# Moving the inner sums of the keys' seventh product to the end of the opening's queue

## Chip, cores and metric

The kernel runs on one core of one Trainium2 chip. The metric is the device time of one execution in microseconds (us); the times given are the median of the runs of one kernel, and one further execution is taken apart by the profiler.

## What is computed

`x` holds 8 images of 512 channels by 1024 positions (fp32). Two attention layers follow each other, each with a residual sum:

```python
# layer 0: LayerNorm over channels, 8 heads of 64
q, k, v = (xn @ W.T + b for each of Wq, Wk, Wv)
x = (softmax(q k^T / 8) v) @ Wo.T + bo + x
# layer 1: GroupNorm of 32 groups, one head of 512
q, k, v = (W h + b for each of wq, wk, wv)
x = x + wp (softmax(q^T k / sqrt(512)) v) + bp
```

The 512x512 weights are the same for all images.

## The kernel before

**Products.** The 512-wide matrix products are done as 2x2 blocks in Winograd's form of Strassen's scheme, with seven block products in place of eight. `STEPS` lists the seven; each needs a block of the weights or a sum of blocks (S1 to S4). Some products are done so twice: the block itself is cut into 2x2 again ("deep"), and then its own inner sums are needed. For the weights these inner sums are made once, in the opening (the work before the first attention), by `save_deep_later`. It queues five pieces for each group of slots: four VectorE additions and one transfer, on the queue of GpSimd (POOL), of the result to DRAM (`saved_deep`). Groups 0, 1 and 2 hold two slots each, and group 3 only one, slot "22", which is the operand of the seventh product. From the second image on `load_deep` reads these sums back; for the keys (`"k"`) that is all four groups.

**The queue of small work.** Instructions are laid down in the order in which the Python code runs; within one engine they run in that order. Small work is put into a queue, `side`, with `later`. A `Product` step lays down its matmuls (`multiply`), then takes `pieces` pieces off the front of `side` (`tick`), then lays down its evictions (`leave`). `Pair.values` takes one piece for each of its eight key blocks. `until` takes pieces until a condition holds. So the place of a piece in `side` decides where its instructions stand among those of the main work.

**The next image's layer norm.** `LayerNorm(1)` is cut into pieces by a generator, `steps`: two sums over channels on VectorE (`lns`), a matmul with ones for the mean (L1045, into a PSUM bank), four ScalarE copies to `mu` (L1063), four subtractions (L1107), four squares on ScalarE (L1111), sums of the squares (`lnq`), a matmul for the variance (L1045, into a PSUM bank named `var`), a VectorE transpose that reads this bank out (`vart`, L990), the inverse root, its spread (`rstd`, L995) and four multiplications (L1135). `queue` puts the first piece at the end of `side`; each piece then puts its successor at place 1, that is, behind one other piece:

```python
side.insert(len(side) if self.waiting == "now" else 1, piece)
```

**The opening around the change.** The keys of image 0 (`project("k0")`) are followed by its queries (`project("q0")`, two units of seven steps), its values (`project_v("v0")`, two units of seven steps), and then the first two score stages. With the queries, the keys' inner sums are queued (20 pieces), three steps are done, and `ln.queue()` is called; the inner sums of the queries' (`q`), and of two combined weights (`a`, `m`), are queued ahead of the values.

**Scores and values of layer 0.** For a pair of heads, `Pair.scores` lays down, for each of eight key blocks, two matmuls (L1294) that fill 128x1024 of PSUM, an exponential on ScalarE (`p`, L1297), and a running sum on VectorE (`sum`, L1301 and L1303). `Pair.values` multiplies with the values (L1312, into `acc`), and the result is copied out on ScalarE (L1316). Two pairs' scores are followed by two pairs' values. `PairSums.take` folds the sums with transfers on POOL (L1005, L1001).

**Buffers.** PSUM is split into three wide tiles of two banks (`wide_psum`) and two single ones (`bank`). Three of a double pair's sixteen score blocks use the two single banks, one for each half, in place of a wide tile:

```python
if m + self.c % 2 * NM in (7, 11, 15):
    s = None
    parts = [bank(f"s{i}_{self.tag}_{m}") for i in range(2)]
```

The single banks also hold the `y` of each product unit, the mean and the variance. Tiles of 128x1024 in SBUF come from a pool of 46 (`big_tile`), tiles of 128x512 from a pool of 9 (`half_tile`). A tile comes free when the last instruction laid down that uses it is done.

Of the kernel before, what the change touches and what calls it, by code (L numbers as in the profile page):

```python
# [71 lines left out]
def fast_path(ctx: ExitStack, tc: tile.TileContext, x: bass.AP, vecs: dict, weights: dict, out: bass.AP,  # L72
# [32 lines left out]
    def big_tile(name):  # L105
        return big.tile([P, S], F32, tag="b", name=name)

    def half_tile(name):
        return half.tile([P, HB], F32, tag="h", name=name)
# [40 lines left out]
    def load_x(b):  # L150
        t = {}
        for k in range(NH):
            for j in range(2):
                t[j, k] = block(f"x_{b}_{j}{k}")
                nc.sync.dma_start(out=t[j, k], in_=x[b, ts(j, CB), ts(k, HB)].rearrange("(a p) t -> p a t", p=P))
        return t
# [57 lines left out]
    def deep_tile(n, b, g):  # L214
        return big_tile(f"w_{n}_{b}_{g}_deep").rearrange("p (s i o) -> p s i o", s=2, i=4)
# [10 lines left out]
    def save_deep_later(n, w, groups=range(3)):  # L226

        def sums(g):
            s = len(SLOTS[2 * g : 2 * g + 2])
            left, right = w[g][:, :s, :, :P], w[g][:, :s, :, P:]  # L230
            made = []

            def one(i, l, r, op):
                if not made:
                    made.append(deep_tile(n, "first", g))
                d = made[0][:, :s]
                l, r = (d[:, :, x] if isinstance(x, int) else x for x in (l, r))
                nc.vector.tensor_tensor(d[:, :, i], l, r, op)

            later(lambda: one(0, right[:, :, 0], right[:, :, 1], ALU.add),  # L240
                  lambda: one(2, left[:, :, 0], right[:, :, 0], ALU.subtract),
                  lambda: one(1, 0, left[:, :, 0], ALU.subtract),
                  lambda: one(3, left[:, :, 1], 1, ALU.subtract),
                  lambda: nc.gpsimd.dma_start(out=saved_deep[n][:, g, :s], in_=made[0][:, :s]))

        for g in groups:
            sums(g)
# [35 lines left out]
    def first_w(n):  # L283
        w = weight_tiles(f"{n}_first")
        load_blocks(n + "0", w)
        return w
# [7 lines left out]
    wk_now, wq_now = first_w("k"), first_w("q")  # L294
# [57 lines left out]
    def later(*work):  # L352
        side.extend(work)
# [116 lines left out]
    def banks_of(tag, r, shared, own="x"):  # L470

        def banks(to):
            if to == "y":
                return bank(f"y_{tag}_{r}")
            if shared is None or to in own:
                return wide_psum(f"{to}_{tag}_{r}")[:, :HB]
            if to not in shared:
                shared[to] = wide_psum(f"{to}_{tag}")
            return shared[to][:, ts(r, HB)]
        return banks  # L480
# [9 lines left out]
    def token_part(r):  # L490

        def part(dst, a, b, opens):
            for m in range(2):
                for k in range(2):
                    nc.tensor.matmul(dst[:, ts(m, CB)], b[:, k, ts(2 * r + m, P)], a[:, k, :],  # L495
                                     start=(opens and m == 0 and k == 0), stop=(k == 1), skip_group_check=True)
        return part
# [458 lines left out]
    def project_v(tag, w, h, apart=False):  # L956


        res, shared = {}, None if apart else {}

        def unit(r):
            def dest(i, k):
                if (i, k) not in res:
                    res[i, k] = big_tile(f"{tag}_{i}{k}")
                return res[i, k][:, ts(r, HB)]

            return Product(f"{tag}_{r}", w, h, token_part(r), plain_shift, dest, banks_of(tag, r, shared))
        return [unit(r) for r in range(2)], res
# [728 lines left out]
    with tc.manual_schedule(engines=ORDERED):  # L1697
# [56 lines left out]

        units, qt = project("q0", wq_now, bias_of("bq0"), hb)
        ln.xt = load_x(1)
        save_deep_later("k", wk_now, range(4))
        units[0].step(3)
        ln.queue()
        for u in units:  # L1760
# [2 lines left out]
        save_deep_later("q", wq_now)  # L1763
        save_deep_later("a", wa, (1, 2))
        save_deep_later("m", wm, (1, 2))
        units, vts = project_v("v0", wv_now, hb)
        units[0].pieces = 0
        units[0].step(1)
# [3 lines left out]
        for b in range(B):  # L1772
# [13 lines left out]
            for i in range(HEADS):  # L1786
# [3 lines left out]
                p = pairs[i]  # L1790
# [524 lines left out]
@with_exitstack  # L2315
def attn_block_x2(ctx: ExitStack, tc: tile.TileContext, x: bass.AP, vecs: dict, weights: dict, out: bass.AP):
    nc = tc.nc
    keep = ctx.enter_context(tc.tile_pool(name="keep", bufs=1))
    flag = keep.tile([1, 1], I32, tag="flag", name="flag")
    fast_path(tc, x, vecs, weights, out, flag)  # L2320
    left = nc.values_load(flag[0:1, 0:1])
    with tc.If(left > 0):
        general_path(tc, x, vecs, weights, out)
# [39 lines left out]
```

## Time and profile before

| | |
|---|---|
| median of 3 runs | 2793.82 us (2792.96 to 2796.17) |
| profiled execution, its own time | 2795.6 us |
| its span in the trace | 2793.9 us, so 1.7 us lie around the span |
| TensorE busy | 2777.7 us (99% of the span) |
| VectorE, ScalarE, GpSimd busy | 2177.2, 1274.0, 523.1 us |
| mean granted TensorE clock | 0.998 |

The trace gives each instruction's start, its duration and what released it. PE is TensorE's matmuls, PEld its weight loads, DVE is VectorE, ACT ScalarE, POOL GpSimd, SP the engine that issues most loads. Ends of matmuls are modelled, so intervals are best taken from start to start. Every fp32 matmul is shown as two rows. Engines that are not the bottleneck may be idle at no cost.

### The profile page before, as it was taken

The page shows a single profiled execution, that of the slowest core. Times are in us where ns is not written, and L with a number is a line of the kernel's source. Part 1 is how long each engine was busy: PE and PEld are TensorE (multiplying, and loading weights), DVE is VectorE, ACT ScalarE, POOL GpSimd, SP SyncE. Part 2 cuts the span into 40 slices and gives each one's busy share as a digit, 9 for nine tenths or more (in the row PEclk, how much of TensorE's full clock was granted, in tenths as well). Part 3 has the DMA queues.
Part 4 walks back from the last instruction along what each step waited for, and adds up shares of the span by engine and source line. Part 5 has one row for each costly group of instructions (what it writes and reads, how often), then busy time and mean ns, then how long its engine had stood idle before and what let it go on. Part 6 is the DMA issues. An engine that isn't in the chain of part 4 may idle for free.

```text
span 2793.9 us, 32794 instructions
## 1 busy us (share of the span) xinstructions
PE 2777.7 (99%) x11385; PEld 1637.5 (59%) x11385; DVE 2177.2 (78%) x3128; ACT 1274.0 (46%) x2152; POOL 523.1 (19%) x719
## 2 busy tenths in 40 slices
PE   9999999999999999999999999999999999999999
PEld 4534766357663585536855468644676447763375
DVE  6687798678877788777887778777887778757776
ACT  4463435634357243562436534365344743336342
POOL 2022012210222102221022210222012210122001
PEclk9999999999999999999999999999999999999999
DMA  8235458344673537636475364744548434282223
GB/s 310 100 101 132 133 128 215 76 125 125 162 189 67 156 109 189 150 74 176 111 194 117 83 192 118 197 88 105 165 121 208 97 103 132 61 215 63 66 91 96
DMA packets 143550, 372.96 MB, mean 133 GB/s; under 512 B 20064, under 2 KB 24464, under 8 KB 143376
## 3 DMA queue, kind: packets, MB, share of 16 engines
q0 software_dynamic: 58208, 141.34, 26.9%
q1 hardware_dynamic: 81040, 216.56, 22.3%
q10 hardware_dynamic: 4128, 12.87, 1.5%
q8 instruction: 92, 1.51, 0.2%
q14 instruction: 82, 0.67, 0.1%
HBM read 208.43 MB, written 64.75 MB: 98 GB/s over the span
## 4 chain that ended last, share of the span: by engine, by line
PE 99%; ACT 0%; DMA 0%; DVE 0%; issue 0%; SPq 0%; DVEq 0%
PE acc L1312 16%; PE s L1294 16%; PE x_o L511 8%; PE s L1460 7%; PE x_v L495 4%; PE y_o L511 4%; PE x_out L486 4%; PE y_s L1460 3%; PE y_v L495 2%; PE c_vm L858 2%; PE s L1495 2%; PE y_out L486 2%; PE z_o L511 2%; PE x_k L609 2%; PE x_q L609 2%; PE c_qa L732 2%
## 5 line engine op out<-in xcount | busy, mean ns | idle before, releaser
L1303 DVE TENSOR_TENSOR sum<-sum,p 128x1024 f32<-128x1024 f32 x384 | 470.4, 1225 | 40.4 <-ACT p L1297 2.2
L1297 ACT ACTIVATE p<-s 128x1024 f32<-128x1024 f32 (+1 forms) x608 | 479.3, 980 | 20.2 <-PE s L1294 20.2
L1312 PE MATMUL acc<-p,v_again 128*64 128x512 f32 x1792 | 390.9, 594 | 0.0
L1312 PEld LDWEIGHTS acc<-p,v_again 128*64 128x64 f32 x1792 | 126.1, 137 | 261.3 <-issue 236.7
L1001 POOL DMA_DIRECT2D fold<-sum x312 | 207.4, 752 | 338.1 <-DMA sum<-sum 212.1
L1294 PE MATMUL s<-q,k 64*128 64x512 f32 x1152 | 253.7, 593 | 4.5 <-ACT p L1297 4.5
L1301 DVE TENSOR_TENSOR sum<-p,p 128x1024 f32<-128x1024 f32 x64 | 78.1, 1221 | 156.0 <-ACT p L1297 156.0
L1294 PE MATMUL s<-q_lower,k_lower 64*128 64x512 f32 x896 | 196.1, 592 | 0.0
L1294 PEld LDWEIGHTS s<-q,k 64*128 64x128 f32 x1152 | 109.8, 186 | 144.8 <-issue 86.0
L1294 PEld LDWEIGHTS s<-q_lower,k_lower 64*128 64x128 f32 x896 | 85.4, 186 | 110.4 <-issue 68.3
L1005 POOL DMA_DIRECT2D sum<-sum x78 | 63.5, 839 | 425.2 <-DVE sum L1303 199.3
L1316 ACT COPY o<-acc 128x512 f32<-128x512 f32 x63 | 36.9, 586 | 221.0 <-PE acc L1312 220.8
L1500 DVE TENSOR_TENSOR p<-p,p 128x1024 f32<-128x1024 f32 x96 | 112.9, 1216 | 6.3 <-ACT p L516 6.3
L511 PE MATMUL x_o<-T_p,S_vm 128*128 128x512 f32 x256 | 114.0, 592 | 0.0
L516 ACT COPY u(0, 0)_v<-x_v 128x512 f32<-128x512 f32 x16 | 9.4, 586 | 187.6 <-PE x_v L495 187.6
L486 PE MATMUL x_out<-T_o,w_o 128*128 128x512 f32 x192 | 89.2, 594 | 0.0
L511 PEld LDWEIGHTS x_o<-T_p,S_vm 128*128 128x128 f32 x256 | 48.6, 190 | 60.7 <-issue 60.7
L1358 ACT COPY rr<-r 32x16 f32<-32x16 f32 x256 | 53.2, 208 | 63.1 <-DVE r L1261 59.7
L495 PE MATMUL x_v<-w_v,T_h 128*128 128x256 f32 x336 | 80.0, 381 | 0.0
L995 DVE STREAM_TRANSPOSE rden<-rr 128x512 f32<-128x512 f32 (+1 forms) x72 | 53.4, 758 | 24.0 <-ACT rr L1603 15.2
L495 PEld LDWEIGHTS x_v<-w_v,T_h 128*128 128x128 f32 x336 | 63.3, 190 | 11.3 <-issue 3.3
L1448 ACT ACTIVATE p<-p 128x1024 f32<-128x1024 f32 x64 | 65.3, 1061 | 0.0
(680 smaller groups left out, 5609.5 us busy)
## 6 DMA issues: line engine op xcount, KB each, us to landing
sum<-sum POOLq DMA_DIRECT2D x78, 256.0 KB, 3.4
fold<-sum POOLq DMA_DIRECT2D x312, 64.0 KB, 2.3
x<-in_x_dram SPq DMA_DIRECT2D x32, 512.0 KB, 5.8
xr<-in_x_dram SPq DMA_DIRECT2D x64, 256.0 KB, 4.3
x_away<-x SPq DMA_DIRECT2D x32, 512.0 KB, 3.2
v_away<-v SPq DMA_DIRECT2D x28, 512.0 KB, 2.8
v_again<-v_away SPq DMA_DIRECT2D x28, 512.0 KB, 7.1
w_o<-saved_o SPq DMA_DIRECT2D x24, 512.0 KB, 5.1
```

The source lines that it names most:

```text
L486: nc.tensor.matmul(dst, a[:, k, ts(r, P)], b[:, k, :], start=(opens and k == 0), stop=(k == 1), skip_group_check=True)
L495: nc.tensor.matmul(dst[:, ts(m, CB)], b[:, k, ts(2 * r + m, P)], a[:, k, :], start=(opens and m == 0 and k == 0), stop=(k == 1), skip_grou ...
L511: nc.tensor.matmul(dst, a[:, r, ts(m, P)], b[m // 2][:, m % 2, :], start=(opens and m == 0), stop=(m == NM // 2 - 1), skip_group_check=True)
L609: nc.tensor.matmul(dst[:, ts(s, CB)], a[s], b[s], start=(opens and s == 0), stop=True, skip_group_check=True)
L1001: nc.gpsimd.dma_start(out=f[ts(q + i, BL), :], in_=t[ts(n, BL), ts(i, HB)], accum_op=ALU.add if n else ALU.bypass)
L1294: nc.tensor.matmul(parts[i], self.k[m // 4][r, ts(m % 4, P)], self.q[r, :], start=True, stop=True)
L1297: nc.scalar.activation(dst, src, AF.Exp, scale=1.0 / float(D) ** 0.5)
L1301: nc.vector.tensor_add(self.sum, self.p[0], p)
L1303: nc.vector.tensor_add(self.sum, self.sum, p)
L1312: nc.tensor.matmul(acc[i * D : (i + 1) * D, :], value_of(self.vt, m, self.c * P + i * D, D), self.p[m][:, ts(i, HB)], start=(m == 0), stop ...
L1460: nc.tensor.matmul(dst[:, ts(c, CB)], x[0][:, ts(c, P)], a[0], start=(opens and c == 0), stop=True, skip_group_check=True)
L1500: nc.vector.tensor_add(wide(t), wide(t), wide(x))
```

## The change

The keys' group 3 is taken out of the first call of `save_deep_later`, and a call of its own is put behind those of `q`, `a` and `m`. Its sums go into a half tile (128x512, from the pool of 9) where before they took half of a tile from the pool of 46. The same four additions and the same transfer are done.

```diff
@@ save_deep_later
                 if not made:
-                    made.append(deep_tile(n, "first", g))
+                    made.append(deep_tile(n, "first", g) if s == 2 else
+                                half_tile(f"w_{n}_first_{g}_deep").rearrange("p (s i o) -> p s i o", s=1, i=4))
                 d = made[0][:, :s]
@@ the opening
         ln.xt = load_x(1)
-        save_deep_later("k", wk_now, range(4))
+        save_deep_later("k", wk_now)
         units[0].step(3)
         ln.queue()
...
         save_deep_later("q", wq_now)
         save_deep_later("a", wa, (1, 2))
         save_deep_later("m", wm, (1, 2))
+        save_deep_later("k", wk_now, (3,))
         units, vts = project_v("v0", wv_now, hb)
```

## Prediction

> **What bounds the kernel now.** I read the page's busy times and chain first: TensorE is at work for 99% of the span, so an edit can gain only where TensorE waits or runs slowly.
>
> ```profile
> PE 2777.7 (99%) x11385; PEld 1637.5 (59%) x11385; DVE 2177.2 (78%) x3128; ACT 1274.0 (46%) x2152; POOL 523.1 (19%) x719
> PE 99%; ACT 0%; DMA 0%; DVE 0%; issue 0%; SPq 0%; DVEq 0%
> ```
>
> The waits of TensorE come next (total, times, longest). Nearly half of the 9.4 us that they hold in the whole span is one kind: scores that wait for an exponential.
>
> ```profile
> PE s L1294 <- ACT p L1297: 4.5, 3, 1.7
> PE pst_k L306 <- DMA w_k<-in_L_conv_wk_dram: 2.0, 1, 2.0
> ```
>
> TensorE's timeline puts all three into the first score stage, at 131, 136 and 141 us. The next score stages have none.
>
> ```profile
> 122.67 1.08 PE L1045 MATMUL var<-lnq,ones_c 128*64 128x512 f32 x4
> 123.68 7.13 PE L1294 MATMUL s<-q,k 64*128 64x512 f32 x30
> 131.92 3.70 PE L1294 MATMUL s<-q,k 64*128 64x512 f32 x16 [1.11 <-ACT p L1297]
> 137.33 3.70 PE L1294 MATMUL s<-q,k 64*128 64x512 f32 x16 [1.71 <-ACT p L1297]
> 142.75 1.12 PE L1294 MATMUL s<-q,k 64*128 64x512 f32 x2 [1.71 <-ACT p L1297]
> 143.80 15.65 PE L1312 MATMUL acc<-p,v 128*64 128x512 f32 x64
> 159.38 14.00 PE L1294 MATMUL s<-q,k 64*128 64x512 f32 x64
> ```
>
> A block is four rows, and the waits stand after rows 30, 46 and 62 of 64: in the middle of blocks 8, 12 and 16, the three that use the single banks, between their halves. VectorE's timeline says why only one bank is free. The variance is written at 122.67, but its reader comes only behind both pairs' running sums:
>
> ```profile
> 144.54 1.23 DVE L1303 TENSOR_TENSOR sum<-sum,p 128x1024 f32<-128x1024 f32 x1 [0.20 <-ACT p L1297]
> 145.68 0.71 DVE L990 STREAM_TRANSPOSE vart<-var 128x512 f32<-128x512 f32 x1
> ```
>
> So `var` holds one of two banks through the stage, and the second half of a block must wait for the exponential of its first half. The same work by stage (length; busy PE, PEld, DVE, ACT, POOL; granted clock; DMA):
>
> ```profile
> 123.68:143.80 20.12, 15.59 (x66) 6.20 (x65) 15.30 (x13) 14.90 (x18) 2.13 (x4) 1.00 0.32 99
> 143.80:159.38 15.58, 15.58 (x65) 4.89 (x65) 11.33 (x21) 1.72 (x4) 5.95 (x9) 0.89 0.53 127
> 159.38:173.31 13.93, 13.93 (x66) 6.10 (x64) 10.16 (x13) 13.34 (x17) 0.00 (x0) 1.00 0.00 1
> 173.31:187.20 13.89, 13.89 (x67) 4.51 (x65) 13.14 (x20) 4.30 (x13) 4.39 (x7) 1.00 0.45 78
> ...
> 144.00:146.00 2.00, 2.00 (x6) 0.48 (x4) 1.80 (x3) 0.50 (x1) 1.17 (x2) 0.53 0.49 53
> 146.00:148.00 2.00, 2.00 (x8) 0.62 (x6) 1.56 (x7) 0.54 (x2) 0.80 (x1) 0.62 0.41 49
> ```
>
> The first scores take 20.12 us against 13.93, and the values behind them 15.58 against 13.89: right after the waits the clock is granted at about half for some 4 us.
>
> [...]
>
> **The change part by part.**
>
> *Taken from the front of the queue.* Five pieces go: three additions of 0.283 us and one of 0.292 (128x128 rows of L238), 1.14 us of VectorE, and the POOL transfer issued at 90.80. None bounds TensorE. What counts is that the layer norm of image 1 stands behind twelve pieces where it stood behind seventeen, so all its pieces come five earlier. The instruction order of the changed program shows it: the mean's matmul moves ahead of four product steps (one y, x of the queries, x, z of the values), the variance's ahead of the last five steps of the values, and `vart` to before the scores. The number of matmuls is unchanged.
>
> *Are the moved pieces ready in time?* Worked from start times of before. VectorE begins `lns` at 89.49 instead of 90.42; four additions at paces of 1.15, 0.60, 1.15 and 0.68 end at 93.1. TensorE reaches the mean after the step at 92.05, plus 1.72: 93.8. Spare: 0.7. Image 1 was loaded from 32 us on, long landed. The `mu` copies start 1.15 after the mean (100.74 to 101.89 before), at 95.0, and the first subtraction 1.20 later at 96.2. ScalarE's squares now stand ahead of the copy `u(0, 0)_v`: squares at 97.4 and 99.2 (it waits for the second subtraction), the queries' copy, then `u(0, 0)_v`, done at 101.4. TensorE needs it at 93.8 + 1.1 (mean) + 4x1.72 = 101.8. Spare: 0.4, the tightest place. Further on, `v` block (1, 1) is added at 107.9 against 108.6, and `lnq` ends at 110.2 against 113.9. `var` ends at 115.0, `vart` at 115.8: eight us before the scores. I take 0 for new waits; the bounds are 0 and 1.5, as a late square holds back ScalarE's queue. Scores still start at 123.7, since the steps before them are the same ones.
>
> *The gain.* With both banks free the first stage is like the next: 20.12 - 13.93 = 6.19. Without the pauses I expect no half clock: 15.58 - 13.89 = 1.69. Sum 7.88. The next score stage then starts at 151.5 instead of 159.4.
>
> *What must keep up.* The sums are paced by VectorE (7.87 / 6 = 1.31 each): 14 of them from 126.8 to 145.2. Behind them stand three multiplications and one inner sum (4.0) and eight of `a` (3.4): 152.6. The next sums can start at 151.5 + 3.15 = 154.7. Spare 2. On POOL the first pair's folds stay; the second pair's end at 156.2 (issue of the last at 153.9, 2.3 to land). The changed program gives the buffer of that pair's sum to the exponential of pair 3's fifth block, due at 151.5 + 1.2 + 12x0.876 = 163.2 (ScalarE took 7.01 for eight). Spare 7.
>
> *Put at the end.* The four additions run at about 178. VectorE is busy 13.14 of 13.89 there, but three additions of `a` (1.25) leave that stage as these 1.14 come, and the stage behind has 3.8 to spare (10.16 of 13.93). The transfer (a POOL issue took 0.55) now stands behind those of `m` and ahead of pair 4's fold, where POOL sat idle 7.35. The half tile's next user is an eviction of the next image's values, past 230. No SP issue moves. I take 0 for it; bounds 0 and 0.5. If VectorE's slack were gone, 1.14 would fall on the sums. A later scaling (`rden`) stands behind two more pairs' sums; its reader is the projection after 242. Later images have the same order as before.
>
> **Rivals.**
>
> *Part of it.* The waits go, but the clock still dips, or the projections pay up to 1.5: gain 4.5 to 6.4, that is 2787.4 to 2789.3. For it: 0.4 us of spare is little. Against it: the other score stages all run at clock 1.00.
>
> *Slower.* The wait at 163.2: if the four folds of the second sum land late, ScalarE stops at pair 3's fifth exponential, and scores behind it. Each us past 163.2 costs one; it takes 171.1, fifteen us later than worked, to eat the gain. At 20 us late (176.2) it costs 13.0 - 7.9 = 5.1: 2798.9. For it: one fold waited 3.0 us for a transfer at 191. Against it: the longest chain seen, from the sum's issue at 183.05 to landing, is 12 us, and mine has 10.5 and 7 to spare.
>
> *Nothing happens.* ScalarE is the pace, not the bank: it was busy 14.90 of 20.12. Then 2793.8. Against it: 13.93 us are enough for the same exponentials one stage later.
>
> **How the numbers follow.** About 0.2% (5.6 us) is what a measurement of this kernel can tell from no change. Forecast as worked: 0.80; part of it: 0.12, of which 0.05 within 5.6 us; nothing: 0.04; slower: 0.04. So faster 0.87, same 0.09, slower 0.04. The profiled execution (2795.6, span 2793.9) would become 2787.7 and 2786.0. It is 1.8 above the median of 2793.82, which becomes 2785.9. The runs spread from 0.9 below to 2.4 above the median: 7.9 gained and 2 of spread give 2783.9; the worst of "part of it" gives 2789.3.
>
> **What would show it.** TensorE's waits without the line of scores on exponentials; the first score stage at 14 us; granted clock 1.00 in the values behind it; `vart` near 115. A wait of x of the values on ScalarE's copy near 102 would show the tight place failing; a wait on a fold near 163, the slower rival. I am wrong if the waits go and the stage stays at 18 us or more.

## The result, and the profile after

The changed kernel takes 2787.57 us (median of 12 runs, 2786.68 to 2789.31) against 2793.97 us for the kernel before (12 runs, 2792.96 to 2796.17): a ratio of 0.9976, 95% interval 0.9967 to 0.9985, or 6.4 us by the medians. Its profiled execution took 2787.6 us, with a span of 2785.9, against 2795.6 and 2793.9 before: 8.0 us. All lines of the new file stand one further down than before up to the place where the group was moved (scores L1295, values L1313, `vart` L991).

TensorE's busy time on the page, and then its waits in the whole span (total, times, longest):

```profile
PE 2774.7 (100%) x11385; PEld 1636.9 (59%) x11385; DVE 2177.2 (78%) x3128; ACT 1273.1 (46%) x2152; POOL 522.2 (19%) x719
```

```profile
PE pst_k L307 <- DMA w_k<-in_L_conv_wk_dram: 2.1, 1, 2.1
PE ps_first L1701 <- DVE checks L142: 1.3, 1, 1.3
PE pst_q L307 <- DMA w_q<-in_L_conv_wq_dram: 0.7, 1, 0.7
```

The line of scores that wait for an exponential, 4.5 us before, is gone; the longest that remain wait for the first weights and for the first tile of the program. TensorE did not compute less, its count of 11385 is the same. The timeline of TensorE, and below it VectorE's reader of the bank:

```profile
122.05 1.89 PE L496 MATMUL x_v<-w_v_first,T_h 128*128 128x256 f32 x8
123.87 14.00 PE L1295 MATMUL s<-q,k 64*128 64x512 f32 x64
137.81 13.95 PE L1313 MATMUL acc<-p,v 128*64 128x512 f32 x64
151.69 14.00 PE L1295 MATMUL s<-q,k 64*128 64x512 f32 x64
```

```profile
115.18 0.72 DVE L991 STREAM_TRANSPOSE vart<-var 128x512 f32<-128x512 f32 x1 [0.29 <-PE var L1046]
```

All 64 rows of the first score stage now run as one stretch, and the next score stage begins at 151.69 where it began at 159.38: 7.7 us earlier. `vart` is read eight us ahead of the scores and not in the stage behind them. The two stages by windows (length; busy PE, PEld, DVE, ACT, POOL; granted clock; DMA):

```profile
123.87:137.81 13.94, 13.94 (x66) 6.11 (x65) 11.01 (x11) 13.35 (x17) 0.87 (x1) 1.00 0.23 76
137.81:151.69 13.88, 13.88 (x66) 4.50 (x65) 12.97 (x17) 2.78 (x5) 3.42 (x5) 1.00 0.55 106
```

13.94 in place of 20.12, and 13.88 in place of 15.58: 6.18 and 1.70 us, at a clock of 1.00 throughout.

The three idle times in the timeline of before, 1.11, 1.71 and 1.71 us, add up to 4.53 of these 6.18. The timeline models the ends of matmuls, so these idle times come out short. Taken from start to start, at the 0.218 us a row of the stage now (13.94 / 64), the three stops cost 1.7, 1.9 and 1.9 us, and 0.6 more lie between the last rows and the first of the values.

### The profile page after: what moved, and what is told of

It is laid out like the page before. It is cut to its first block, busy times and chain, and to the rows that moved or that the text cites. A ratio compares the mean times of both kernels' runs of the same rounds, so it can differ in the third digit from the quotient of the medians.

```text
span 2785.9 us, 32795 instructions
## 1 busy us (share of the span) xinstructions
PE 2774.7 (100%) x11385; PEld 1636.9 (59%) x11385; DVE 2177.2 (78%) x3128; ACT 1273.1 (46%) x2152; POOL 522.2 (19%) x719
## 4 chain that ended last, share of the span: by engine, by line
PE 99%; DMA 0%; DVE 0%; issue 0%; ACT 0%; SPq 0%; DVEq 0%
PE s L1295 16%; PE acc L1313 16%; PE x_o L512 8%; PE s L1461 7%; PE x_v L496 4%; PE y_o L512 4%; PE x_out L487 4%; PE y_s L1461 3%; PE y_v L496 2%; PE s L1496 2%; PE c_vm L859 2%; PE y_out L487 2%; PE z_o L512 2%; PE x_q L610 2%; PE x_k L610 2%; PE c_qa L733 2%
## 5 line engine op out<-in xcount | busy, mean ns | idle before, releaser
L1313 PE MATMUL acc<-p,v_again 128*64 128x512 f32 x1792 | 390.9, 594 | 0.0
L1313 PEld LDWEIGHTS acc<-p,v_again 128*64 128x64 f32 x1792 | 126.1, 137 | 261.3 <-issue 236.7
L1295 PE MATMUL s<-q,k 64*128 64x512 f32 x1152 | 252.1, 592 | 0.0
L1295 PE MATMUL s<-q_lower,k_lower 64*128 64x512 f32 x896 | 196.1, 592 | 0.0
L1295 PEld LDWEIGHTS s<-q,k 64*128 64x128 f32 x1152 | 109.7, 186 | 138.2 <-issue 84.9
L1295 PEld LDWEIGHTS s<-q_lower,k_lower 64*128 64x128 f32 x896 | 85.4, 186 | 110.5 <-issue 68.5
```

The costliest lines, as they stand in the source:

```text
L1295: nc.tensor.matmul(parts[i], self.k[m // 4][r, ts(m % 4, P)], self.q[r, :], start=True, stop=True)
L1313: nc.tensor.matmul(acc[i * D : (i + 1) * D, :], value_of(self.vt, m, self.c * P + i * D, D), self.p[m][:, ts(i, HB)], start=(m == 0), stop ...
```

## The experiments

The theory is that `var`, waiting in one of the two single banks for VectorE, made the scores stop, and that the change helps only because it brings `vart` ahead of the scores. It competes with three other readings: that fewer additions or transfers in the opening help by themselves, that the half tile helps, and that ScalarE's pace makes the waits. A further question is when the half clock comes.

**The moved group without the earlier layer norm.** Another five pieces, the queries' first group, fill the place that the keys' group has left:

```diff
         save_deep_later("k", wk_now)
+        save_deep_later("q", wq_now, (0,))
         units[0].step(3)
         ln.queue()
...
-        save_deep_later("q", wq_now)
+        save_deep_later("q", wq_now, (1, 2))
```

> The kernel after, with the first group of q's inner sums (five pieces too) put where k's fourth group stood: k's four additions and its transfer stay at the end of the queue and stay in a half tile, but the LayerNorm's pieces come no earlier than in the kernel before, and VectorE reads the variance's bank behind both pairs' sums again. Theory (the bank held by var stops TensorE in the first score stage): the gain is gone, 2793 to 2796 us, the first score stage takes about 20 us and the waits on the scores' two late blocks are back. Rival (the gain comes from taking k's additions and transfer out of the opening, or from the half tile): 2787 to 2789 us.

Measured: 2794.07 us median, ratio to before 1.0002 (0.9994 to 1.001). The waits are back to the hundredth, in TensorE's timeline:

```profile
131.93 3.70 PE L1295 MATMUL s<-q,k 64*128 64x512 f32 x16 [1.11 <-ACT p L1298]
137.35 3.70 PE L1295 MATMUL s<-q,k 64*128 64x512 f32 x16 [1.71 <-ACT p L1298]
142.76 1.35 PE L1295 MATMUL s<-q,k 64*128 64x512 f32 x2 [1.71 <-ACT p L1298]
```

Everything that the change does to the keys' seventh operand is still in this kernel, and nothing is gained. What counts is the place of the layer norm.

**The read alone.** The kernel before with one line:

```diff
+        until(lambda: hasattr(ln, "var"))
         for b in range(B):
```

> The kernel before with one line more: just ahead of the loop over images the queue is worked off up to and including the read of the variance's bank. No sum of the weights moves against the LayerNorm, no tile changes; only the read of the bank comes ahead of the first scores. Theory: nearly the whole gain, 2787 to 2789 us, first score stage 14 us, half clock gone. Rival (the moved additions matter): 2793 to 2796 us. A second rival (reading early makes VectorE late for the values' last products): above 2790 us with a new wait of TensorE ahead of the scores.

Measured: 2787.44 us median (12 runs, 2786.81 to 2787.86), ratio 0.9976 (0.9967 to 0.9985). No wait of the scores is left, though VectorE reads the bank only after the scores have begun (they start at 123.97):

```profile
124.08 0.72 DVE L990 STREAM_TRANSPOSE vart<-var 128x512 f32<-128x512 f32 x1 [1.72 <-PE var L1045]
```

The scores run in one stretch, with the same nineteen exponentials as before. TensorE's and ScalarE's timelines:

```profile
123.97 14.00 PE L1294 MATMUL s<-q,k 64*128 64x512 f32 x64
```

```profile
125.14 14.96 ACT L1297 ACTIVATE p<-s 128x1024 f32<-128x1024 f32 x19 [1.49 <-PE s L1294]
```

The whole gain comes without moving one sum of the weights. ScalarE's pace is no limit either: its exponentials take 14.96 us back to back and end in the values stage, and TensorE doesn't wait for them. The read need not be early; it must be done by block 8, the first that takes the single banks (the two runs with a later read, below, keep the wait of 1.11 us there).

**The tile's size.** Two kernels: the change with the keys' fourth group in a whole tile as before, and the kernel before with only the half tile.

```diff
-                    made.append(deep_tile(n, "first", g) if s == 2 else
-                                half_tile(f"w_{n}_first_{g}_deep").rearrange("p (s i o) -> p s i o", s=1, i=4))
+                    made.append(deep_tile(n, "first", g))
```

> The kernel after, with the moved sums in a whole tile as before in place of a half one. Theory: the tile's size is worth nothing by itself, 2787 to 2788.5 us. Rival (the half tile is needed, since the big tile is held at the end of the opening where another tile waits for it): 2790 us or more, with a wait on a buffer behind the moved sums between 140 and 190 us.

> The kernel before with the half tile alone: the keys' fourth group is summed at its old place, into a half tile. Theory: as before, 2793 to 2796 us, with the three waits in the first score stage unchanged. Rival (the freed half of a big tile is what lets something start earlier): a gain of over 2 us.

Measured: 2788.05 us (15 runs, 2787.04 to 2789.30; ratio 0.9978, 0.9970 to 0.9985) for the move in a whole tile, and 2793.99 us (ratio 1.0001, 0.9992 to 1.0009) for the half tile alone, with its three waits at the same places. The first has no wait of the scores left. The move is the gain. Whether the half tile is worth the 0.5 us between 2788.05 and 2787.57 these runs don't tell: the ranges overlap.

**The same gain by another road.** The order of before is kept, and blocks 8, 12 and 16 of the first score stage take wide tiles:

```diff
-                if m + self.c % 2 * NM in (7, 11, 15):
+                if m + self.c % 2 * NM in (7, 11, 15) and self.tag not in ("0_0_0", "0_0_1"):
```

> The kernel before with the order untouched; in the first score stage alone the blocks 8, 12 and 16 take a two-bank tile like all others, so that no score needs the single banks, one of which var holds. Theory: the waits go by this road as well, since the bank was what they waited for: 2787 to 2789.5 us, first score stage 14 to 15 us. Rival (ScalarE's or VectorE's pace makes the waits): the waits stay in another place, 2792 us or more.

Measured: 2787.73 us (11 runs, 2787.03 to 2789.01), ratio 0.9977 (0.9968 to 0.9986). The timelines of TensorE and of VectorE:

```profile
123.28 14.38 PE L1294 MATMUL s<-q,k 64*128 64x512 f32 x64
137.59 13.95 PE L1312 MATMUL acc<-p,v 128*64 128x512 f32 x64
```

```profile
144.65 0.71 DVE L990 STREAM_TRANSPOSE vart<-var 128x512 f32<-128x512 f32 x1
```

`var` keeps its bank until 144.65, behind all sums as in the kernel before, and nobody waits, because nobody wants that bank. ScalarE does the same sixteen blocks without holding TensorE up, though here in sixteen instructions in place of nineteen; that nineteen don't hold it up either was shown by the read alone.

**The read at places between.** The kernel before, with the same `until` between the two pairs' scores, and, in a second kernel, behind the fifth block of the second pair:

```diff
+                if b == 0 and i == 1:
+                    until(lambda: hasattr(ln, "var"))
                 pairs[i].scores(range(NM))
```

```diff
+                if m == 4 and self.tag == "0_0_1":
+                    until(lambda: hasattr(ln, "var"))
```

> The kernel before with the variance's bank read between the two pairs of the first score stage: behind the first pair's sum in place of behind both. By before's own times VectorE ends the first pair's sum near 136 us and would free the bank near 137. Theory: the first wait (1.1 us) stays, the second (1.7 us, from 135.6 to 137.3) ends at most with the bank's release, the third (1.7 us) is gone: 1.7 to 2.6 us gained by the waits, and up to 1.7 us more if the clock stays whole; 2789.5 to 2792.5 us. Rival (what counts is only that something of the LayerNorm comes ahead of the scores, not the bank): as before, 2793 to 2796 us, or all of it, 2787 to 2788 us.

> The kernel before with the variance's bank read still later than in the run with the read between the pairs: behind the fifth block of the second pair, whose sum VectorE by before's own trace ends near 140.9 us in a stage that starts at 123.7, so the bank comes free near 141.5 us. Theory: the first two waits stay (1.1 and 1.7 us), the third, which was 141.0 to 142.7 us, shrinks to 0.3 to 0.8 us; 0.9 to 1.4 us gained by it. If the half clock belongs to the third wait's full length, its share goes too, and the executions agree within 1.5 us: 2791.8 to 2792.8 us. Rival on the clock (two full waits are enough for it): 2792.8 to 2793.6 us with the spread of before, 3.8 us.

Measured with the read between the pairs: 2790.98 us (21 runs, 2790.27 to 2791.74), ratio 0.9988 (0.9982 to 0.9995). Its waits, then TensorE's timeline:

```profile
PE s L1294 <- ACT p L1297: 1.1, 1, 1.1
PE s L1294 <- DVE vart L990: 1.1, 1, 1.1
```

```profile
130.99 3.70 PE L1294 MATMUL s<-q,k 64*128 64x512 f32 x16 [1.11 <-ACT p L1297]
135.78 4.55 PE L1294 MATMUL s<-q,k 64*128 64x512 f32 x18 [1.08 <-DVE vart L990]
```

Here the trace names `vart`: the second wait ends at 135.78, when it has read the bank, and the third is gone. In the kernel before, the same wait bore the exponential's name alone. `vart` stood behind all scores there, so the second half of the block had to take the bank of its own first half, and the trace names what freed that one, not what held the other. The stage takes 17.51 us (122.75 to 140.26), between 20.12 and 13.94.

With the read behind the fifth block: 2792.90 us (13 runs, 2792.34 to 2794.70), ratio 0.9995 (0.9987 to 1.0004). The interval includes no change. The third wait shrank only from 1.71 to 1.32, by 0.39, where a gain of 0.9 to 1.4 was expected:

```profile
PE s L1294 <- ACT p L1297: 2.8, 2, 1.7
PE s L1294 <- DVE vart L990: 1.3, 1, 1.3
```

The stage that this ends takes 19.74 us (122.94 to 142.68), 0.4 less than before. The expectation had misread the start: in before's trace the fifth block's sum ends at 141.7, two additions (2.55 us) behind 139.12, and not at 140.9. Nor do the executions agree within 1.5 us: they spread over 2.4, and the median lies just outside the theory's range and inside the rival's. The profile below is at full clock, as the theory wanted, but one profile doesn't decide between them. The median is 1.65 us below the 2794.55 of the 17 runs of before made alongside, more than the wait explains; what is known of the clock, below, would account for it.

**Ten pieces earlier in place of five.** The keys' third group goes to the end too:

```diff
-        save_deep_later("k", wk_now)
+        save_deep_later("k", wk_now, (0, 1))
...
-        save_deep_later("k", wk_now, (3,))
+        save_deep_later("k", wk_now, (2, 3))
```

> The kernel after with the keys' third group moved to the end as well: the LayerNorm comes ten pieces earlier than before in place of five, and its bank is read some ten us earlier still. Theory: nothing more to be had there, since no wait on the bank is left: 2787 to 2788.5 us. Rival (each sum moved out of the opening is worth something): 2781 to 2786 us. Second rival (the LayerNorm's additions now stand ahead of the queries' last products, and TensorE waits for them or for the mean's input): 2789 to 2793 us with a new wait between 80 and 95 us.

Measured: 2789.20 us (13 runs, 2787.85 to 2790.54), ratio 0.9981 (0.9973 to 0.9989): 1.6 us above the change, though the two intervals overlap. TensorE has a new wait in the queries, and ScalarE's timeline shows for what:

```profile
PE x_q L487 <- ACT u(0, 1)_q L530: 1.3, 1, 1.3
```

```profile
90.90 2.36 ACT L1064 COPY mu<-mean 64x512 f32<-64x512 f32 x4 [3.79 <-PE mean L1046]
93.28 0.69 ACT L530 ACTIVATE u(0, 1)_q<-x_q,vecs 128x512 f32<-128x512 f32 x1
```

Four copies of the mean, 2.36 us, now stand in ScalarE's queue directly ahead of an eviction that TensorE needs. The eviction's product had ended at 89.8, and the eviction starts at 93.28, as the copies end. So nothing more was to be had from an earlier read. The second rival came true by its number and by the place of its wait (94.03), but not by its cause: it expected TensorE to wait for the LayerNorm's additions or for the mean's input.

**The kernel before, once more.**

> The kernel before once more, for a second look at the half clock of 144 to 148 us: if it follows from the waits, it stands at the same place again and costs 1 to 2.5 us; if it came by chance in the first look, the values stage behind the first scores takes 13.9 us and the span is about 2792 us.

Measured: one execution of 2796.13 us, span 2794.4. The values stage by windows:

```profile
143.91:159.49 15.58, 15.58 (x66) 4.91 (x65) 11.33 (x21) 1.73 (x4) 6.19 (x9) 0.89 0.50 127
```

The half clock stands where it stood, at the same cost, 15.58 against 13.88. The profiles of the two kernels that keep all three waits (the other group in its place, the half tile alone) show it too, with 0.76 between 143 and 150 us. The profile with the shortened third wait doesn't:

```profile
142.68:156.56 13.88, 13.88 (x65) 4.50 (x64) 11.37 (x20) 1.61 (x4) 6.20 (x9) 1.00 0.43 89
```

But the four profiled executions with the half clock took 2795.4 to 2796.1 us, all above the medians near 2794 of their kernels, so not every execution can have it. Before's first 12 runs fall into seven of 2792.96 to 2794.12 and five of 2795.09 to 2796.17, with medians 1.70 us apart, which is what the half clock costs in the trace; the runs with the read behind the fifth block into ten of 2792.34 to 2793.30 (the profiled one, 2792.89, at full clock) and three of 2794.56 to 2794.70. In the later 42 runs of before the two groups run into one another. Without three long waits the spread is smaller: a standard deviation of 0.3 to 0.6 us in the change and the kernels with its time or with the read between the pairs, 0.8 in the one with two groups moved and in the one with the read behind the fifth block, and 1.0 to 1.2 in those with all three.

Each run's mean granted clock, to three digits, points the same way. Of the 98 later runs of before, 29 read 1.000, with a median of 2793.37 us; 69 read less, with a median of 2794.93. In the change and in the three kernels that have its time, the same two readings lie at most 0.3 us apart. The readings can't sort every run: 4 us at 0.57, the clock from 144 to 148 us in the trace of before, lower the mean over 2794 us by only 0.0006 (an estimate from these three numbers). With the read behind the fifth block, the median of the lower ten is 2792.84, which is 0.43 below the 2793.27 of the six runs of before at 1.000 alongside; the stage was 0.38 shorter. That the half clock comes in a part of the executions is thus inferred from times and mean clocks; no execution of before at full clock was profiled.

## Why the prediction was right, and where it missed

The sign, the mechanism and the range were right; the median missed by 1.7 us (2785.9 predicted, 2787.57 measured), and none of the twelve runs reached it (the lowest is 2786.68).

*The waits.* Predicted 6.19 us from the two stage lengths, measured 6.18. That the bank was the cause is shown from three sides: the read alone brings all of it, score tiles that avoid the bank bring all of it with the read still late, and a read in between brings part of it.

*The clock, the term that missed.* 1.69 us were predicted for the half clock and 1.70 are seen between the profiled executions. For its own execution the sum held: 2787.7 and a span of 2786.0 predicted, 2787.6 and 2785.9 measured. The step that failed is the subtraction of the same 7.88 from the median. The profiled execution stood 1.8 us above the median, and the prediction noted this without asking why; by the grouping above, seven of the twelve runs of before do not pay the clock, so that the median holds little of it. From the lower group's median, 2793.68, the waits alone give 2787.49, and 2787.57 was measured.

*The rival "part of it".* 2787.4 to 2789.3 by number holds the measured median, but not by its mechanism: the clock didn't dip and no new wait came. It was the base, not the gain, that was sized wrongly. The time alone could not have told the two apart; the trace does.

*The rival "nothing happens".* It was answered with 13.93 us being enough for the exponentials. That reading is not right: they take 14.96 us in the stage it names (from 160.56 on) and run over into the values. The conclusion holds, since TensorE doesn't wait for them there.

*The tight place.* ScalarE's copy was predicted to end at 101.4 for a product that starts at 101.8. ScalarE's and TensorE's timelines:

```profile
99.20 1.06 ACT L1112 ACTIVATE sq<-x 128x1024 f32<-128x1024 f32 x1 [0.68 <-DVE x L1108]
100.28 0.69 ACT L530 ACTIVATE q<-x_q,vecs 128x512 f32<-128x512 f32 x1
100.86 0.58 ACT L517 COPY u(0, 0)_v<-x_v 128x512 f32<-128x512 f32 x1
```

```profile
101.85 1.89 PE L496 MATMUL x_v<-w_v_first,T_h 128*128 128x256 f32 x8
```

The copy ends at 101.44 and the product starts at 101.85 with no wait: spare 0.41, as worked. The kernel with ten pieces shows how narrow it is: there such a place fails by 1.29 us.

*The other pieces.* The mean came at 93.85 (93.8 predicted), `vart` ended at 115.9 (115.8), VectorE's last addition ahead of the next sums at 152.4 (152.6), the four moved additions ran at 177.65 to 178.66 (178). The scores began 0.2 us later than predicted (123.87). The moved transfer was issued at 183.67, with 9.05 idle us of POOL behind it, and no wait of TensorE follows from it.

*The slower rival.* Its spare was 7 us and is less. On POOL, the second pair's folds:

```profile
146.24 0.80 POOL L1006 DMA_DIRECT2D sum<-sum  x1 [1.70 <-issue]
152.94 1.06 POOL L1002 DMA_DIRECT2D fold<-sum  x2 [5.89 <-DMA sum<-sum]
155.09 1.61 POOL L1002 DMA_DIRECT2D fold<-sum  x2 [1.10 <-DMA fold<-sum]
```

The sum's transfer took 6.4 us to land (4.1 before), so the last fold was issued near 156 and not at 153.9. Between 144 and 154 us SyncE's loads of the next values' weights moved 0.79 MB beside it, where 0.26 MB were moved in 144 to 152 before; that this is the reason was not tried. ScalarE ran all the exponentials of that stage in one stretch, so the remaining spare of some 5 us covered it. The fifth block of pair 3 came at 163.8 where 163.2 was worked out.

## What to carry to other kernels

When an engine waits in the middle of a block that uses two buffers, ask what else holds a buffer of that pool and where its last reader stands in the reader's queue; the releaser that the trace names is that of the buffer the block got, and need not be what holds the other (in the kernel before it named the exponential for all 4.5 us, while `var` held the other bank). Here the cheapest remedy was to place that read just ahead of the first use of the pool: one line did all that the reordering of sums did, and reading still earlier put four copies ahead of an eviction and lost about 1.6 us. Subtract a gain that was read in one profiled execution from that execution's time, and before carrying it to the median ask what sets the two apart.

## What the hardware did that was not expected

Three waits of 1.1, 1.7 and 1.7 us within 12 us, none of them longer than 1.71 as the profile lists them, are followed in four profiled executions of four by about 4 us at half clock (0.57 from 144 to 148 us in before, 0.76 from 143 to 150 us in each of the four), which costs 1.7 us more (15.58 us for the values stage in before and in its second profile, 13.88 in the changed kernel). With the third wait at 1.32 us, or with two waits of 1.1 us, the profile shows the full clock (1.00 in the values stage behind), and the times suggest that the half clock then comes rarely or not at all. But each of these was profiled once, and the kernel with all three waits seems to run some of its executions at full clock too, so what length or number of waits it takes is not shown.
